# Image staging, constant loads and weight preparation moved in a four-layer pre-activation convolution kernel

## The chip, the core and the metric

The kernel runs on one core of a Trainium2 chip. The core has a tensor engine (PE, with its weight load PEld), a vector engine (DVE), a scalar engine (ACT), a general engine (POOL) and a sync engine (SP); SP, ACT and POOL can issue DMAs, each on a queue of its own. Each engine runs its own instructions in program order and waits on semaphores for the others. The metric is the device time of one execution in microseconds (us), lower is better.

## The reference

The input is x of 8 images, 128 channels, 96 x 96 pixels, float32. Four layers follow each other; each is the input plus a layer of its group norm (32 groups of 4 channels, statistics over 4 x 96 x 96 values of one image):

```python
x = x + dcnv4(_gn(x))            # layer 0
x = x + conv3x3(_gn(x), kernel)  # layer 1, 128 -> 128 channels
x = x + dwconv(ste_sign(v), w) + dwconv(v, ste_sign(w))   # layer 2, v = _gn(x), depthwise 3 x 3
x = x + scan(_gn(x))             # layer 3
```

Layer 0 is a deformable convolution: a depthwise 3 x 3 convolution of the normed image (x1), a norm of x1 over all channels and pixels, a gelu, and a projection that gives two offsets and a mask for each of 8 groups and 9 taps; each tap is then sampled bilinearly at its offset, weighted by the mask and summed. Layer 3 goes through the rows of an image from top to bottom: each row plus the last result goes through a 9-wide convolution over the row, a bias and a relu, and is the next carry.

## The kernel before

**Order of the work.** The layer-0 stage and the stage of layers 1 and 2 are not written in order. They make tasks for a planner (`Plan`, L96 on): a task has an engine, an estimated cost, what it depends on, a due time (`prio`), buffers that it uses and a `lag` until its result is there. `order` then simulates the engines: an idle engine takes the ready task with the lowest due time whose buffers are free. The instructions are emitted in that order, and on the chip each engine keeps it, whatever the real durations are. The engines carry on from one stage to the next without a barrier; only data, reused memory and the branch hold them.

**Start (L253 to L485).** `load_const` loads constants through ACT's DMA queue in the order of the code: 8 of them, then the small matrices `idq` and `gmq`, four more, and then for layer 0 the selection matrices `sel`, `shift`, `omb`, `omq` (8 loads), and the depthwise weights `dwq`, `dwbq`, `gnwq`, `gnbq`. DVE makes 18 diagonal matrices `dwd` from `idq` and `dwq`. POOL sets the edges of two image tiles `xqs` to zero.

**Layer 0 (L486 to L948).** The 128 partitions hold two row halves of 64 channels each, the channels' other half lies beside it (index j), so one image is a tile of 52 rows x 2 x 100 columns with a zero edge of 2; a row inside it is 96 values, 384 bytes, with gaps between rows. Two tiles alternate between images. `load_rows` (L483) issues four DMAs for a piece of rows: 24 DMAs for image 0, 48 for each later one, all on SP. Then `image` plans: `bn_stats` on DVE (L545, 24 of them), the aggregate, the means on PE, coefficients on DVE with a square root on ACT (L555 to L563, L329), and norms in place on ACT (L597, 26 pieces of 4 rows or less). The image is worked off in 12 bands of 4 rows per half. For a band the depthwise convolution gives x1: 36 matmuls on PE (L628), or, for bands 3, 5, 7 and 9 of image 0, 18 instructions on DVE (L620, L622); ACT takes it out of PSUM (L648), squares it for the statistics (L657), and SP stores it in DRAM (`x1d`, L665 and L669). When all 12 bands are done, the coefficients of x1's norm follow (L689 to L696, with a matmul by `amean`).

Then 12 chunks follow. For one chunk: x1 is loaded back (L731), gelu (L738), the projections (PE, L748), their eviction `o` (ACT, L767), tent functions of the offsets `h` (L757, L780), a check whether an offset is over 1 (`beyond`, L788, L793), the mask product (DVE, L809) and the residual row load `acc` (L821). Then come 9 weight products `wt` (POOL, L852) and 25 shifts, each with a selection (`select`, PE, L862, 4 matmuls into a PSUM buffer), a product with the shifted image (DVE, L879) and an addition, which is on PE into `ps_s` (L839), on POOL (L897) or on DVE (L886) by a fixed list. ACT writes the result y (L906) with sums for the next norm (L914), SP stores it (L919). PSUM has a pool "w" of three buffers that the bands, projections, selections and coefficients share, and one buffer `ps_s`. A band of the next image and its norms are planned among the chunks of the image before; for image 1 among those of image 0, and its bands start early. The loads of image 1 wait for the weights of layer 1: `conv_weights` (L502) loads `k1` into tile 1 of `xqs` and makes `km1` by six DVE sums, before image 1 may be loaded there.

**The flag (L949 to L959).** After the planned part, three DVE operations and a PE transpose reduce `beyond` to a flag, which is read into a register, and a branch (`tc.If`) follows. It guards a slow path for offsets over 1, which is not taken here.

**Layers 1 and 2 (L1093 to L1560).** The tiles of this stage have names with a suffix C, in chunks of 8 rows. Per image and chunk: y is loaded (L1241), normed (L1252), transformed over row pairs on POOL (`d`, L1259), multiplied with `km1` on PE (L1272, four products into two PSUM buffers `pv_C`) and summed into v on DVE (L1288 to L1308) with statistics (L1317). `v_coefs`, the norm of v (L1546) and `tap_chunk` follow for layer 2: nine taps are split over PE (L1385, L1392), DVE (L1406) and POOL (L1423), `xq` on POOL (L1362), the result `o` (L1467) is stored to `x3` (L1473), and `out_coefs` (L1494 to L1521) makes the coefficients of the last norm. `tap_weights` (L1132) makes sign and tanh of the taps on ACT and 20 small DVE operations; `late_weights` (L1153) loads the row weights `k3s` and makes `km` by six DVE sums. The due times of both lie in the first image: at 80 and 20 x 2 x `NCH`, but with no dependence, so the planner may take them when DVE or SP is idle before.

**Layer 3 (L1565 to L1692).** Suffix D, in groups of 4 rows of all images: `x3` is loaded in 24 groups of 1536 KB (`load`, L1626; groups 0 and 1 on POOL's queue before anything else, later ones on SP), normed (L1634), and each row in two halves of 4 images goes through a copy or sum (L1656, L1658), three transforms `tr` (L1660 to L1662), 36 matmuls (L1675), `m2` (L1683), `pair` (L1598 to L1601), a relu (L1614) and a POOL addition (L1615). The row result is the next row's carry, two halves alternate.

Memory is given to pools in order. A stage's pool lies where the closed pools of the stage before lay, and the first write to a piece waits for the last use of what lay there.

Of the kernel before, what the change touches and what calls it, by code (L numbers as in the profile page):

```python
# [11 lines left out]
F32 = mybir.dt.float32  # L12
I32 = mybir.dt.int32
AF = mybir.ActivationFunctionType
ALU = mybir.AluOpType
# [198 lines left out]
def kernel(  # L214
# [35 lines left out]
    def half(j):  # L250
        return slice(j * HC, (j + 1) * HC)
# [3 lines left out]

    def load_const(ap, shape, name):
        t = const.tile(shape, F32, name=name)
        nc.scalar.dma_start(t[:], ap)
        return t

    ident = load_const(c_ident, [P, P], "ident")
    gmean = load_const(c_gmean, [P, P], "gmean")
    amean = load_const(c_amean, [P, P], "amean")
    dww = load_const(dw_w, [P, K2], "dww")
    dwb = load_const(dw_b, [P, 1], "dwb")
    gnw = load_const(gn_w, [P, 1], "gnw")
    gnb = load_const(gn_b, [P, 1], "gnb")
    omw = load_const(om_wT, [P, 3 * GK], "omw")
# [8 lines left out]
    nc.vector.tensor_scalar(gmq[:], gmq[:], 1.0 / NB, None, ALU.mult)  # L277
    w2s = load_const(w2, [P, K2], "w2s")
    b3s = load_const(b3, [P, 1], "b3s")
    alx = load_const(alpha_x.unsqueeze(0).to_broadcast([P, 1]), [P, 1], "alx")  # L280
    alw = load_const(alpha_w.unsqueeze(0).to_broadcast([P, 1]), [P, 1], "alw")
    eps = const.tile([P, 1], F32, name="eps")
# [129 lines left out]
    with ExitStack() as ph:  # L412
# [16 lines left out]
        for j in range(NB):  # L429
            rows = slice(j * HC, j * HC + GR)  # L430
            taps = slice(j * GR, (j + 1) * GR)
            nc.scalar.dma_start(sel[rows, :, :], c_sel[taps, :, half(j)])
            nc.scalar.dma_start(shift[rows, :], c_shift[taps, :])
            with nc.allow_non_contiguous_dma(reason="216 biases, one per partition"):
                nc.scalar.dma_start(omb[rows, :], om_b[:, taps].rearrange("k r -> r k"))
            for b in range(NB):
                for m in range(NB):
                    nc.scalar.dma_start(
                        omq[half(b), j, :, m * HC : m * HC + GR],
                        om_wT[half(j), :].rearrange("c (k r) -> c k r", k=3)[:, :, m * GR : (m + 1) * GR],  # L440
                    )
            nc.scalar.dma_start(dwq[half(j), :, :], dw_w.rearrange("(j c) t -> c j t", c=HC))
            with nc.allow_non_contiguous_dma(reason="128 values of each"):
                nc.scalar.dma_start(dwbq[half(j), :], dw_b.rearrange("(j c) o -> c (j o)", c=HC))
                nc.scalar.dma_start(gnwq[half(j), :], gn_w.rearrange("(j c) o -> c (j o)", c=HC))
                nc.scalar.dma_start(gnbq[half(j), :], gn_b.rearrange("(j c) o -> c (j o)", c=HC))
# [5 lines left out]
        for xq in xqs:  # L452
            nc.gpsimd.memset(xq[:, :RS, :, :], 0.0)
            nc.gpsimd.memset(xq[:, XR - RS :, :, :], 0.0)
            nc.gpsimd.memset(xq[:, RS : XR - RS, :, :RS], 0.0)
            nc.gpsimd.memset(xq[:, RS : XR - RS, :, RS + W :], 0.0)
        nmx = wp.tile([P, N], F32, name="nmx")
# [18 lines left out]
        def load_rows(i, lo, hi):  # L476

            for b in range(NB):

                a, z = (max(lo, RS), hi) if b == 0 else (lo, min(hi, XR - RS))  # L480
                top = b * HB - RS
                for j in range(NB):
                    nc.sync.dma_start(  # L483
                        xqs[i % 2][half(b), a:z, j, RS : RS + W], x[i, half(j), top + a : top + z, :]
                    )  # L485
# [16 lines left out]
        def conv_weights(at):  # L502
# [10 lines left out]
                [], at, lag=4.0,  # L513
# [11 lines left out]
            return t  # L525

        def image(i, at):
# [13 lines left out]
            for m in range(NST):  # L541
                for j in range(NB):
                    stats.append(plan.task(
                        "DVE", 0.49,
                        lambda m=m, j=j: nc.vector.bn_stats(  # L545
                            st[:, j, m, :], xq[:, RS + m * RB : RS + (m + 1) * RB, j, RS : RS + W]
                        ),
                        [loads[m], loads[min(m + 1, NST - 1)]], at - 20 + m,
                    ))
# [45 lines left out]
            def norm(parts, lo, hi, j):  # L595
                rows = xq[parts, lo:hi, j, RS : RS + W]
                nc.scalar.activation(  # L597
                    rows, rows, AF.Identity, bias=bi[parts, j : j + 1], scale=sc[parts, j : j + 1]
                )
# [5 lines left out]

            st1 = small["st1"][:].rearrange("p (k c) -> p k c", k=2)
# [86 lines left out]
            def aggr1():  # L693
# [13 lines left out]
                [t], when, uses=[b3],  # L707
# [15 lines left out]
        def chunk(i, c, at, made):  # L723
# [37 lines left out]
            for k in (1, 0):  # L761
# [29 lines left out]
                plan.task(  # L791
# [5 lines left out]
                )  # L797
# [136 lines left out]

        squares = {}
        weights = conv_weights(-STEP * NST)
        made = {0: image(0, -STEP * NST)}
        for i in range(N):
            for c in range(NST):
                at = STEP * (i * NST + c)  # L940
                chunk(i, c, at, made[i])
            plan.task("DVE", 0.7, lambda i=i: y_stats(i), squares[i], at + 2 * STEP)
            if i + 1 < N:
                made[i + 1] = image(i + 1, STEP * i * NST)
        with tc.manual_schedule():
            plan.emit()


            m1 = sp.tile([P, 1], F32, name="m1")  # L949
            nc.vector.tensor_reduce(m1[:], beyond[:], AX.X, ALU.max)  # L950
            pt = plan.pools["s"].tiles[0]
            nc.tensor.transpose(pt[:1, 0, :P], m1[:], ident[:])
            m2 = sp.tile([1, 1], F32, name="m2")
            nc.vector.tensor_reduce(m2[:], pt[:1, 0, :P], AX.X, ALU.max)
            nc.vector.tensor_scalar(flag[:], m2[:], 0.0, None, ALU.is_gt)
# [146 lines left out]
    with ExitStack() as ph:  # L1102
        wp = ph.enter_context(tc.tile_pool(name="wpC", bufs=1))
# [7 lines left out]
        for name, n, shape in (  # L1111
# [4 lines left out]
            tiles = [wp.tile(shape, F32, name=f"{name}C{k}") for k in range(n)]  # L1116
# [15 lines left out]
        def tap_weights(at):  # L1132
# [13 lines left out]
            s = plan.task("ACT", 1.9, signs, [], at)  # L1146
# [6 lines left out]
        def late_weights(at):  # L1153

            ld = plan.task("SP", 0.6, lambda: nc.sync.dma_start(k3s[:], k3), [], at, lag=4.0)
# [373 lines left out]
        weights = tap_weights(20 * 4)  # L1529
        late_weights(20 * 2 * NCH)  # L1530
        for i in range(N):
# [6 lines left out]
            done = v_coefs(i, stats + ends.get(i - 2, []) + (weights if i == 0 else []), 20 * (i + 1) * NCH)  # L1538
            made[i] = [done]
            norms = []  # L1540
# [25 lines left out]
    with ExitStack() as ph:  # L1566

        wp = ph.enter_context(tc.tile_pool(name="wpD", bufs=1))
        xts = [wp.tile([P, N, LG, W], F32, name=f"xtD{g}") for g in range(3)]
        xgs = [wp.tile([P, N, LG, W], F32, name=f"xgD{g}") for g in range(3)]  # L1570
# [68 lines left out]
        with tc.manual_schedule():  # L1639
            for g in range(2):  # L1640
                load(g, nc.gpsimd)
# [122 lines left out]
```

## Time and profile before

| what | value |
| --- | --- |
| median of 3 runs | 5604.98 us (5604.57 to 5605.74) |
| the profiled execution | 5606.45 us, its span 5604.7 us |
| mean granted TensorE clock | 0.990 |
| PE, PEld | 96%, 54% of the span busy |
| DVE, ACT, POOL | 86%, 60%, 81% busy |
| layer-0 stage, by the last y | 0 to 3467.6 us |
| layers 1 and 2, by the last PE work | 3476.9 to 4822.1 us |
| layer 3 | from there to the end |

The profile is of one execution. A group row reads: line, engine, operation, output <- input (partitions x elements), count, then busy time and mean duration, and the idle time just before with what ended it. In a timeline a row has a start and a duration in us and a count if like instructions follow each other. In a row of a stretch each engine has its busy us with the number of its instructions, then the granted clock (1.00 is full), the DMA engines' share and the GB/s moved. Durations carry over to another kernel only for the same shape. The busy shares are averages over stages: what a stage is bound by has to be read in the stage.

### The profile page before, as it was taken

What the parts mean: (1) busy time and instruction counts of PE and PEld (TensorE: products, weight loads), DVE (VectorE), ACT (ScalarE), POOL (GpSimd) and SP (SyncE); (2) the same over time, 40 slices, a digit from 0 to 9 for tenths busy, and PEclk for the clock granted to TensorE, in tenths of its full rate; (3) what the DMA queues carried; (4) which work ended last, traced back from release to release, by engine and by line L of the source; (5) the groups of instructions that cost most, each with busy time, mean ns of one, the idle gap of its engine ahead of it and who ended that gap; (6) DMA issues with size and microseconds to landing.
All of it is one profiled execution on the core that took longest, in us unless ns stands there. A gap on an engine that the chain in (4) does not pass through costs nothing. (4 is left out here: it accounts for less than half of the span.)

```text
span 5604.7 us, 128829 instructions
## 1 busy us (share of the span) xinstructions
PE 5382.2 (96%) x53049; PEld 3007.8 (54%) x53049; DVE 4839.3 (86%) x6874; ACT 3371.5 (60%) x4816; POOL 4554.4 (81%) x2835
## 2 busy tenths in 40 slices
PE   5899999999999999999999998999999999899999
PEld 2354454454454454454454443545454554699999
DVE  5788888888888888888888998699999998688887
ACT  4656666656766666666666663477787777533333
POOL 0899999999999999999999998699999998422222
PEclk9999999999999999999999999999999999999999
DMA  6121121221212112112111111222222221223232
GB/s 128 48 60 58 54 61 58 56 61 58 56 59 60 54 58 61 55 59 60 46 49 47 43 41 40 61 67 64 66 67 67 65 66 48 83 95 109 94 110 80
DMA packets 423809, 360.65 MB, mean 64 GB/s; under 512 B 251889, under 2 KB 422417, under 8 KB 423217
## 3 DMA queue, kind: packets, MB, share of 16 engines
q1 hardware_dynamic: 390336, 310.33, 19.7%
q10 hardware_dynamic: 32144, 38.87, 2.0%
q8 instruction: 422, 6.91, 0.5%
q0 software_dynamic: 736, 3.15, 0.2%
q14 instruction: 171, 1.39, 0.1%
HBM read 201.26 MB, written 150.99 MB: 63 GB/s over the span
## 5 line engine op out<-in xcount | busy, mean ns | idle before, releaser
L862 PE MATMUL ps_w<-wt,sel 64*64 64x384 f32 x19200 | 1857.1, 488 | 58.7 <-DVE h L809 17.2
L879 DVE TENSOR_TENSOR pr<-ps_w,xq 128x768 f32<-128x768 f32 x1824 | 1670.0, 949 | 209.4 <-PE ps_w L862 158.7
L852 POOL TENSOR_TENSOR wt<-h,h 128x768 f32<-128x768 f32 x864 | 1583.9, 1838 | 262.1 <-DVE h L809 140.3
L897 POOL TENSOR_TENSOR acc<-acc,pr 128x768 f32<-128x768 f32 x882 | 1618.6, 1837 | 72.4 <-DVE pr L879 60.0
L862 PEld LDWEIGHTS ps_w<-wt,sel 64*64 64x64 f32 x19200 | 743.9, 133 | 925.3 <-issue 287.7
L1272 PE MATMUL pv_C<-dC,km 128*128 128x384 f32 x2304 | 776.2, 491 | 11.9 <-POOL dC L1259 5.0
L839 PE MATMUL ps_s<-pr,idq 64*64 64x384 f32 x7536 | 761.6, 484 | 1.7 <-DVE pr L879 1.1
L1406 DVE SCALAR_TENSOR_TENSOR ps_C<-xqC,w2s,ps_C 128x768 f32<-128x768 f32 x674 | 683.8, 1015 | 85.7 <-ACT ps_C L1444 70.9
L767 ACT ACTIVATE o<-ps_w,omb 128x768 f32<-128x768 f32 x192 | 172.7, 899 | 810.9 <-PE ps_w L748 705.8
L1615 POOL TENSOR_TENSOR xtD<-xtD,cr 128x384 f32<-128x384 f32 x192 | 192.0, 1000 | 575.2 <-ACT cr L1614 513.2
L628 PE MATMUL ps_w<-xq,dwd 64*64 64x384 f32 x6624 | 631.3, 487 | 13.3 <-ACT x L648 6.9
L1272 PEld LDWEIGHTS pv_C<-dC,km 128*128 128x128 f32 x2304 | 426.1, 189 | 359.1 <-issue 47.3
L879 DVE TENSOR_TENSOR ps_w<-ps_w,xq 128x768 f32<-128x768 f32 x480 | 459.9, 958 | 94.7 <-PE ps_w L862 93.5
L757 ACT ACTIVATE h<-o,shift 128x768 f32<-128x768 f32 x576 | 533.1, 926 | 11.1
L780 ACT ACTIVATE h<-h 128x768 f32<-128x768 f32 x576 | 485.8, 843 | 17.4
L1423 POOL TENSOR_TENSOR ptC<-ptC,ptC 128x768 f32<-128x768 f32 x255 | 476.6, 1869 | 1.1
L839 PEld LDWEIGHTS ps_s<-pr,idq 64*64 64x64 f32 x7536 | 307.3, 133 | 302.7 <-issue 164.3
L886 DVE TENSOR_TENSOR acc<-ps_w,acc 128x768 f32<-128x768 f32 x480 | 456.1, 950 | 6.7
L748 PE MATMUL ps_w<-x1c,omq 64*64 64x384 f32 x4608 | 434.7, 490 | 18.3 <-DVE pr L879 14.9
L628 PEld LDWEIGHTS ps_w<-xq,dwd 64*64 64x64 f32 x6624 | 279.1, 133 | 278.0 <-issue 122.0
L1675 PE MATMUL ps_b<-tr,km 128*128 128x192 f32 x2304 | 407.5, 325 | 16.5 <-DVE tr L1660 16.5
L1675 PE MATMUL ps_a<-tr,km 128*128 128x192 f32 x2304 | 406.2, 324 | 0.0
(198 smaller groups left out, 7165.0 us busy)
## 6 DMA issues: line engine op xcount, KB each, us to landing
ywC<-y SPq DMA_DIRECT2D x80, 480.0 KB, 3.9
acc<-in_x SPq DMA_DIRECT2D x192, 192.0 KB, 3.4
x1c<-x1d SPq DMA_DIRECT2D x192, 192.0 KB, 3.3
y<-y SPq DMA_DIRECT2D x96, 384.0 KB, 3.3
x<-oC SPq DMA_DIRECT2D x192, 192.0 KB, 2.8
out<-xtD ACTq DMA_DIRECT2D x24, 1536.0 KB, 5.7
x1d<-x SPq DMA_DIRECT2D x92, 384.0 KB, 2.8
xtD<-x SPq DMA_DIRECT2D x22, 1536.0 KB, 7.0
```

The source lines that it names most:

```text
L628: nc.tensor.matmul(ps.tile[half(j), b, :FB], dwd[half(b), j, t, :], xq[half(b), r0 : r0 + RB, j, c0 : c0 + W], start=(t == 0), stop=(t == ...
L757: nc.scalar.activation(h, o, AF.Abs, bias=shift[:, k * NR + r : k * NR + r + 1])
L780: lambda h=h: nc.scalar.activation(h.tile[:], h.tile[:], AF.Relu, bias=1.0, scale=-1.0),
L839: nc.tensor.matmul(total.tile[half(j), b, :FB], idq[half(b), :], pr.tile[half(b), j, :], start=first, stop=last)
L852: lambda wt=wt, hy=hy, hx=hx: nc.gpsimd.tensor_tensor(wt.tile[:], hy.tile[:], hx.tile[:], ALU.mult),
L862: nc.tensor.matmul(ps.tile[half(b), j, :FB], sel[half(j), n, :], wt.tile[half(j), b, :], start=True, stop=True)
L879: nc.vector.tensor_tensor(view(pr.tile), view(ps.tile), x_s, ALU.mult)
L897: lambda pr=pr, acc2=acc2: nc.gpsimd.tensor_tensor(acc2.tile[:], acc2.tile[:], pr.tile[:], ALU.add),
L1272: nc.tensor.matmul(flat(ps), km1[:, k, x_, :], d.tile[:, k, :, x_ : x_ + W], start=(x_ == 0), stop=(x_ == 2))
L1406: nc.vector.scalar_tensor_tensor(view, rows8(src, t), w[:, t : t + 1], view, ALU.mult, ALU.add)
L1423: lambda a=parts[0], b=pt: nc.gpsimd.tensor_tensor(a.tile[:], a.tile[:], b.tile[:], ALU.add),
L1675: nc.tensor.matmul(ps[:, at_f : at_f + nf], km[:, k, t, :], tr[:, par, :, v : v + HW2], start=(t == 0), stop=(t == NT - 1),)
```

## The change

- Image 0 is loaded without gaps into the memory of tile 1 (`stage`, rows of one half and one j one behind the other), the statistics read it there, and the norms go from there to tile 0. Tile 1's edge is set to zero later, in a POOL task after `conv_weights`, which now waits for the norms of image 0; the loads of image 1 wait for that POOL task.
- 29 constants are no longer loaded through ACT's queue at once; they are SP tasks with a due time just behind image 0's loads. `dwb`, `idq`, `gmq`, `dwq` and `dwbq` stay on ACT. The first `amean` matmul waits for all 29 in the planner.
- The flag's operations become tasks that depend on the last checks, so they go out as soon as those are done.
- In the stage of layers 1 and 2, the tiles yw, d, sg and th get a pool of their own, which is opened first. `tap_weights` waits for the statistics of chunk 3 of image 0, `late_weights` for v's coefficients of image 2 (the third).
- In layer 3, the tiles `xtD0`, `xgD0` and `xtD1` lie in a pool that is opened first, thus where the pool named above was. Group 0 is loaded on POOL's queue, group 1 on SP's.

```diff
+    late = []
+
+    def put_off(to, ap):
+        def load():
+            with nc.allow_non_contiguous_dma(reason="a few values per partition"):
+                nc.sync.dma_start(to, ap)
+
+        late.append(load)
+
     def load_const(ap, shape, name):
         t = const.tile(shape, F32, name=name)
-        nc.scalar.dma_start(t[:], ap)
+        put_off(t[:], ap)
         return t
...
-            nc.scalar.dma_start(sel[rows, :, :], c_sel[taps, :, half(j)])
-            nc.scalar.dma_start(shift[rows, :], c_shift[taps, :])
...
+            put_off(gnwq[half(j), :], gn_w.rearrange("(j c) o -> c (j o)", c=HC))
+            put_off(gnbq[half(j), :], gn_b.rearrange("(j c) o -> c (j o)", c=HC))
+            put_off(shift[rows, :], c_shift[taps, :])
+            put_off(omb[rows, :], om_b[:, taps].rearrange("k r -> r k"))
...
+            put_off(sel[rows, :, :], c_sel[taps, :, half(j)])
...
-        for xq in xqs:
+
+        def zero_edges(xq):
...
+        zero_edges(xqs[0])
+
+        stage = xqs[1][:].rearrange("p r j w -> p (r j w)")[:, : NB * XR * W].rearrange("p (j r w) -> p j r w", j=NB, w=W)
...
+                    rows = x[i, half(j), top + a : top + z, :]
+                    if i == 0:
+                        nc.sync.dma_start(
+                            stage[half(b), j, a:z, :].rearrange("p r w -> p (r w)"), rows.rearrange("p r w -> p (r w)")
+                        )
+                    else:
+                        nc.sync.dma_start(xqs[i % 2][half(b), a:z, j, RS : RS + W], rows)
...
-                [], at, lag=4.0,
+                before, at, lag=4.0,
...
-            return t
+            return t + [plan.task("POOL", 2.5, lambda: zero_edges(xqs[1]), t, at)]
...
-                    rows, rows, AF.Identity, bias=bi[parts, j : j + 1], scale=sc[parts, j : j + 1]
+                    rows,
+                    rows if i else stage[parts, j, lo:hi, :],
...
-                [t], when, uses=[b3],
+                [t, *constants], when, uses=[b3],
...
-        squares = {}
-        weights = conv_weights(-STEP * NST)
-        made = {0: image(0, -STEP * NST)}
+        squares, checks = {}, []
+        constants = [plan.task("SP", 0.6, load, [], -STEP * NST - 29, lag=3.0) for load in late]
+        made, normed = {}, {}
+        made[0] = image(0, -STEP * NST)
+        weights = conv_weights(-STEP * NST + 40, normed[0])
...
+        def set_flag():
+            nc.vector.tensor_reduce(m2[:], pt.tile[:1, 0, :P], AX.X, ALU.max)
+            nc.vector.tensor_scalar(flag[:], m2[:], 0.0, None, ALU.is_gt)
+
+        t = plan.task("DVE", 0.35, lambda: nc.vector.tensor_reduce(m1[:], beyond[:], AX.X, ALU.max), checks, -1e6)
+        t = plan.task("PE", 0.4, lambda: nc.tensor.transpose(pt.tile[:1, 0, :P], m1[:], ident[:]), [t], -1e6, uses=[pt], lag=0.1)
+        plan.task("DVE", 0.45, set_flag, [t], -1e6, uses=[pt])
...
+        wx = ph.enter_context(tc.tile_pool(name="wx", bufs=1))
         wp = ph.enter_context(tc.tile_pool(name="wpC", bufs=1))
...
+            pool = wx if name in ("yw", "d", "sg", "th") else wp
+            tiles = [pool.tile(shape, F32, name=f"{name}C{k}") for k in range(n)]
...
-        weights = tap_weights(20 * 4)
-        late_weights(20 * 2 * NCH)
...
+            weights = tap_weights(20 * 6, stats[CB * 3 : CB * 4]) if i == 0 else []
...
+            if i == min(2, N - 1):
+                late_weights(20 * (i + 1) * NCH + 40, made[i])
...
+        wx = ph.enter_context(tc.tile_pool(name="wxD", bufs=1))
+        size = [P, N, LG, W]
+        xts, xgs = [wx.tile(size, F32, name="xtD0")], [wx.tile(size, F32, name="xgD0")]
+        xts.append(wx.tile(size, F32, name="xtD1"))
...
-            for g in range(2):
-                load(g, nc.gpsimd)
+            load(0, nc.gpsimd)
+            load(1)
```

## The prediction, before the changed kernel ran

> **What bounds the kernel now.** I read the page first (PE busy 96% of the span), then the timeline and the busy times by stretch at the places that the change touches: the first 204 us, the seam at 3470 us and the seam at 4822 us. The chain of waits starts only at 3476 us, so for the beginning I followed the timeline by hand. Columns of the timeline: start, duration, engine, line, what, and in brackets the idle time before it and what ended it.
>
> ```profile
> 0.74 40.46 SPq L483 DMA_DIRECT2D xq<-in_x  x24
> ...
> 47.60 2.40 DVE L545 BATCH_NORM_STATS2 st<-xq 128x6 f32<-128x384 f32 x5 [0.91 <-DMA xq<-in_x]
> ...
> 55.73 12.54 ACT L597 ACTIVATE xq<-xq,bi,sc 64x192 f32<-64x192 f32 x21 [0.89 <-DVE bi L329]
> ```
> The first image takes 24 DMAs of about 192 KB, issued every 1.69 us; the statistics wait for the data until 47.6, and norming starts at 55.73. Call that moment S.
>
> ```profile
> 93.00:96.00 3.00, 0.00 (x0) 0.00 (x0) 2.93 (x6) 2.66 (x6) 0.00 (x0) 0.74 1.02 196
> 96.00:99.00 3.00, 2.80 (x20) 1.23 (x24) 2.93 (x6) 1.18 (x4) 0.00 (x0) 0.50 1.13 280
> ...
> 153.00:156.00 3.00, 0.99 (x8) 0.30 (x8) 1.92 (x2) 2.97 (x5) 0.00 (x0) 0.50 0.00 0
> ```
> Stretches with busy us and counts of PE, PEld, DVE, ACT, POOL, then granted clock, DMA share, GB/s. During the first image's convolution DVE is full; PE falls idle, then runs at half clock. In 147 to 171 (last row) PE is nearly idle at half clock.
>
> ```profile
> 148.67 1.56 PE L862 MATMUL ps_w<-wt,sel 64*64 64x384 f32 x8 [1.09 <-ACT o L767]
> ...
> 203.85 0.81 ACT L906 ACTIVATE y<-ps_s 128x768 f32<-128x768 f32 x1 [6.54 <-PE ps_s L839]
> ```
> The first chunk needs 55.2 us from first select to its y. Later y follow each other by 29.6 to 42 us, with the same pattern in every image: PE and POOL are then full.
>
> ```profile
> 3492.62 7.66 PE L1272 MATMUL pv_C<-dC,km 128*128 128x384 f32 x23 [2.92 <-DVE vn L1288]
> ...
> 4828.64 1.93 POOL L1626 DMA_DIRECT2D xtD<-x  x2 [8.89 <-DVE bi L329]
> ...
> 4832.00:4834.00 2.00, 0.00 (x0) 0.00 (x0) 0.00 (x0) 0.00 (x0) 0.00 (x0) 0.50 1.06 394
> ...
> 4843.66 4.18 PE L1675 MATMUL ps_b<-tr,km 128*128 128x192 f32 x12 [16.53 <-DVE tr L1660]
> ```
> At 3492 PE waits for a DVE that is busy with k3's weights. At the last seam everything waits 11 us for a load that is issued only after the coefficients.
>
> **First image (gain 26.2).** The rows move at 384 B each; 44 to 48 us shows 208 GB/s, while the 1536-byte rows of 4832 reach 394. In contiguous form they are 3072 B or more. The program's order shows that a queue waits for the eighth DMA before, so the landing also depends on what shares these slots: before, tiny constants on ACT's queue (4 omq loads took 5.88 us to issue). They leave. I take the issue interval that 192 KB loads have elsewhere (x1c: 1.24 for 2): 24 x 0.65 + 0.7 = 16.3, and 4.5 to land: 20.8. The Trainium skill (DMA: Bandwidth & Descriptors, "Measured") speaks against this: single transfers of 64 KB reach 138 GB/s, of 1 MB 341, so 192 KB estimated at 200, hence 4.9 MB in 25 us, landing 27. But 208 GB/s was reached here with 384-byte rows, several loads in flight; I keep 20.8, and 27 for the range. DVE then: 18 diagonals end near 13.3, 22 statistics x 0.475 = 10.4, so 23.8; bn_aggr 0.8; the coefficients took 4.2 with the k1 sums in between, about 3.9 without. S = 28.5, rounded up to 29.5 for waits on the ACT constants; landing at 27 would make it 34.6. Gain 55.7 - 29.5 = 26.2 (21 to 27).
>
> The 29 deferred constants go on SP behind the image. Their issues took about 23 us on ACT; from 16.5 that ends at 40, the four residual loads at 43 to 45. SP is next needed for the first x1d store, at S + 13.6 = 43: about covered; beyond that, each us is a us of SP.
>
> **Convolution and the second image (loss 3.6).** Times from S. DVE's band 3 starts at 5.4 as before (61.16 - 55.73), 10.9 a band (1.39 + 16 instructions in 9.55). Band 5 waits for its PSUM buffer until 20.4. The k1 load now waits for the last norm (74.1 before: 18.4) and, behind x1d and x1c on SP, issues near 20; k3's equal load took 6.0, so 26. DVE reaches it at 25.3: stall 0 to 2. Six sums, 2.9. Band 5 ends at 35.7. Bands 7 and 9 then alternate in two PSUM buffers, 22.7: to 58.4, and band 7 is evacuated only at 57.7. PE's last two bands wait for that buffer. They are 144 rows of 0.0807 = 11.6. Rule of the Trainium skill (TensorE: Matmul & The Clock Gate, "What's actually happening"): about 3.4 us idle halves the clock, 3.4 us busy restores it, costing an estimated 1.7. The row at 96.20 had 200 in 18.92, against 16.1 at full clock: 2.8. I take the row's: PE ends at 72.2, against 62.6 before (118.35).
>
> Then evacuation to coefficients as before, 7.7: 79.9. gelu and the first tents need 14.5: 94.5. Meanwhile SP: edges are zeroed on POOL at 38 (8 memsets were 2.35, here half), 48 loads x 0.65 interleaved with x1d stores that wait for evacuations; the last land near 89. Behind them in DVE's queue stand ten statistics, then the mask products: 91. So the first select can start at 96.5. The table loads for Sqrt and back (1.28 each) lie on ACT. Before: 92.9. Loss 3.6 (from -2 to +12).
>
> **First chunk (gain 19.2).** Before, two bands of the second image held two of three PSUM buffers from 122 to 169, since ACT normed late; each select cost 2.64 us. These bands now come after. DVE's work is 25 x 0.93 + 5 x 0.95 + 3 masks 2.9 + 1.2 = 32; with a cold start 36, against 55.2. Bounds 33 and 45.
>
> **Given back (loss 6.5).** Two bands of PE, 11.6 us, move into full chunks; 300 to 400 us holds 1236 PE rows x 0.0807 = 99.8. Chunks 0 to 3 of the first image took 97.97, of the third 103.4: 5.4 less where these bands were done ahead. I take 6.5; bounds 3 and 12. From chunk 5 the program's orders agree up to the last image, so nothing else repeats.
>
> **Seam at 3470 (gain 2).** Three flag operations (0.34, 0.28, 0.14) and a transpose leave the tail: the branch follows y_stats at 3470.74 instead of 3472.0. But DVE does their 0.76 in a full chunk: net 0.5 (0 to 1.3). Without k3 and its sums (6 operations, 3486.4 to 3491.95) DVE releases the product at 3487, and PE's 2.92 goes. Next late would be PE itself. The sums return in the third image, 5.7 us on a DVE with 4 of 50 us free: cost 1 (0 to 4); the 20 small tap operations (3.3 us) fit gaps of 1.25 between products, cost 0.4. Net 1.5 (-2 to 2.9). The inserted table load runs on an ACT that waits anyway; uncovered 1.28.
>
> **Seam at 4822 (gain 11.5).** POOL issues load 0 after its last xq at 4812.2, SP load 1 the same time, ahead of six x stores on SP (2.8 us to land each; oC has two buffers). Three of POOL's last four additions stand behind the DMA, about 1 us; PE needs them at 4820.6: 0.3 late. Both loads land near 4822 at 380 GB/s. The coefficients still end at 4827.9; then norms 2.51, copy and sum 1.0: PE at 4832 instead of 4843.7. PE idles 5 us, so it starts cold as before. Bounds 8 and 13.
>
> **Sum.** 26.2 - 3.6 + 19.2 - 6.5 + 0.5 + 1.5 + 11.5 = 48.8. The profiled execution took 5606.45 (span 5604.7 and 1.75 around it), so 5557.6; the median of the runs lies 1.5 below it: 5556.
>
> **Rivals.**
> 1. *The second image takes back.* Its statistics stand ahead of masks in DVE's queue; loads that land 12 later and a give-back of 12 cost 14 more, a slower landing 5: gain 30, 5575. For: SP's stores stand between its loads. Against: ACT's tents need 94.5 anyway.
> 2. *All cover holds.* First select at 91, chunk 33, give-back 3, S 28.5: 13 to 14 more, 5542.
> 3. *The image doesn't come faster*: eight outstanding DMAs set the pace, not their rows. S stays near 55: gain 23, 5582. Against: 192 KB land in 2.8 to 3.3 us elsewhere.
> 4. *Slower: constants clog SP.* They stand ahead of x1d stores, whose two buffers hold ACT and so every band. At 0.8 us each they are covered; each further 1 us costs 29. Above 2.5 us each (omq's worst is 1.47) the whole 49 are lost; at 3.0, 64 are: 5620.
>
> **How the numbers follow.** Main case 55% (alone 5547 to 5566), rival 1 23%, rival 2 13%, rival 3 4%, rival 4 5%: 2% of it slower, 3% within 0.2% (11 us, about what a measurement of this kernel can tell from no change). Range 5540 to 5580.
>
> **What would show it.** S near 29.5; first select near 126 and first y near 162; the second y's distance over 36; no k3 wait at the seam; PE of the last stage starting about 10 us after the last PE work of the stage before (4822.05 to 4843.66, 21.6, now). Wrong if S exceeds 40, if the image's loads keep 1.69 us, or if SP is still on constants past 50.

## The result, and the profile after

The changed kernel takes 5584.07 us (median of 6 runs, 5575.73 to 5587.12), the kernel before 5603.67 in the same runs (5596.16 to 5605.74): 19.6 us less, ratio 0.9965 with a 95% interval of 0.9954 to 0.9976. The forecast was 5556 with a range up to 5580: the gain has the sign that was forecast and 0.4 of the size. The profiled execution of the changed kernel took 5575.73 (span 5574.0) and is the fastest of the six, so its spans flatter the change by some us; the end of this section says where.

The timeline of the changed kernel's start (start, duration, engine, line, what; in brackets the idle time before it and what ended it):

```profile
0.75 19.20 SPq L499 DMA_DIRECT2D xq<-in_x  x24
...
28.57 2.40 DVE L563 BATCH_NORM_STATS2 st<-xq 128x6 f32<-128x384 f32 x5 [1.05 <-DMA xq<-in_x]
...
35.65 12.49 ACT L618 ACTIVATE xq<-xq,bi,sc 64x192 f32<-64x192 f32 x21 [0.63 <-DVE bi L339]
...
126.67 1.56 PE L888 MATMUL ps_w<-wt,sel 64*64 64x384 f32 x8 [0.43 <-DVE h L835]
...
172.42 0.79 ACT L932 ACTIVATE y<-ps_s 128x768 f32<-128x768 f32 x1
```

The image's 24 DMAs are issued in 19.2 us instead of 40.5, the last statistics run behind 28.57, and the first norm starts at 35.65 (before: 55.73, forecast: 29.5). The first selection comes at 126.67 (148.67; the forecast's path gives 126), the first y at 172.42 (203.85; forecast 162). Up to the last y of image 0 (556.1 against 580.5) the lead shrinks from 31.4 to 24.3 us.

The last seam, first two lines of the kernel before (ACT), then the timeline of the changed kernel:

```profile
4807.56 2.58 ACT L1414 ACTIVATE ptC<-vn,wsg 128x768 f32<-128x768 f32 x3
...
4840.05 4.89 ACT L1634 ACTIVATE xgD<-xtD,bi,sc 128x384 f32<-128x384 f32 x8 [12.62 <-DMA xtD<-x]
```

```profile
4773.64 2.58 ACT L1448 ACTIVATE ptC<-vn,wsg 128x768 f32<-128x768 f32 x3
...
4778.65 1.05 POOL L1665 DMA_DIRECT2D xtD<-x  x1 [0.30 <-POOL xqC L1402]
...
4789.50 4.29 ACT L1673 ACTIVATE xgD<-xtD,bi,sc 128x384 f32<-128x384 f32 x7 [13.28 <-DMA xtD<-x]
4793.70 0.79 ACT L1501 ACTIVATE oC<-ps_C 128x768 f32<-128x768 f32 x1
...
4794.54 3.94 PE L1419 MATMUL ps_C<-vn,dgv 64*64 64x384 f32 x24 [14.81 <-ACT oC L1501]
...
4812.93 4.18 PE L1714 MATMUL ps_b<-tr,km 128*128 128x192 f32 x12 [2.90 <-DVE tr L1699]
```

Read it from below. PE starts the last stage after only 2.9 us of idling (16.53 before), which looks like success. But the stage before it ended late: PE stood 14.81 us, waiting for an eviction oC on ACT, and that eviction came right behind seven norms xgD of the last stage (before, all eight norms came behind the last eviction). These wait 13.28 us for group 0's load, which POOL had issued at 4778.65. The early load itself works; what waits for it stands in front of the stage that is not finished. To compare kernels I take the distance from the group "ptC x3" on ACT, which lies ahead of the tail in all of them, to the last stage's first matmul: 36.1 us before (4807.56 to 4843.66), 39.3 after (4773.64 to 4812.93).

| step, by the two profiles | forecast | measured |
| --- | --- | --- |
| first norm | +26.2 | +20.1 (55.73 to 35.65) |
| from there to the first selection | -3.6 | +1.9 (92.9 to 91.0) |
| first selection to first y | +19.2 | +9.4 (55.18 to 45.75) |
| given back up to image 0's last y | -6.5 | -7.1 |
| last y of layer 0 to ptC x3 | +2.0 | +3.4 (1339.95 to 1336.59) |
| ptC x3 to the last stage | +11.5 | -3.2 (36.1 to 39.3) |
| sum | 48.8 | 24.5 |

What the profiles show beyond the sum, 6.2 us between image 0's last y and layer 0's, is not put down to the change. Layer 0's last y fell at 3437.05 in this profile; in five experiments below that leave layer 0 as in the changed kernel (e1, e2, e7, e10, e13) it fell at 3444.07 to 3447.69. The difference lies where one image follows another, with up to 2.4 us at each such place. There PE waits for DVE ahead of a projection; these are two of these places in the profile of before:

```profile
1439.97 2.84 PE L748 MATMUL ps_w<-x1c,omq 64*64 64x384 f32 x16 [3.61 <-DVE pr L879]
```

```profile
2285.86 1.52 PE L748 MATMUL ps_w<-x1c,omq 64*64 64x384 f32 x16 [0.46 <-DVE pr L879]
```

In the profiles the wait is either about 3.6 us, and then 16 matmuls take 2.84 us (granted clock 0.50 from 1440 to 1442), or half a us, and they take 1.52 (clock 1.00). From the last y of the image to the next it takes 42.0 us in the first case (1425.7 to 1467.7) and 39.7 in the second (2273.8 to 2313.5). Profiles of kernels that are alike in layer 0 so differ by up to 10.6 us; that the spread of one kernel's runs (9.6 and 11.4 us) has the same cause is likely, but not shown. I therefore read the experiments by the stage that they touch, in particular at the last y of image 0, which lies ahead of all these places.

### The profile page after: what moved, and what is told of

It is laid out like the page before. It is cut to its first block, busy times and chain, and to the rows that moved or that the text cites. A ratio compares the mean times of both kernels' runs of the same rounds, so it can differ in the third digit from the quotient of the medians.

```text
span 5574.0 us, 128853 instructions
## 1 busy us (share of the span) xinstructions
PE 5375.0 (96%) x53049; PEld 3013.9 (54%) x53049; DVE 4837.6 (87%) x6874; ACT 3376.3 (61%) x4820; POOL 4552.6 (82%) x2834
## 3 DMA queue, kind: packets, MB, share of 16 engines
q1 hardware_dynamic: 386096, 312.91, 19.6%
```

## Experiments

Times are medians, each beside runs of the kernel before on the same chip (5604.3 to 5605.7). "Image 0's last y" is 580.5 before and 556.1 in the changed kernel.

**Norms held (e1).** Group 0's norms read copies of the coefficients that DVE makes after the last ones.

```diff
+            for to, of in zip(held, (bi3, sc3)):
+                nc.vector.tensor_copy(to[:], of[:])
...
+            bi, sc = held if g == 0 else (bi3, sc3)
```

> The changed kernel, but the eight norms of group 0 of the last stage read copies of the coefficients that are made after the last image's, so that ACT cannot have them ahead of its last evictions. From the eviction group ptC x3 on ACT to the last stage's first matmul it took 36.1 us before (4807.56 to 4843.66) and 39.3 us after the change (4773.64 to 4812.93). Theory A (the queue): seven norms stand in ACT's order ahead of the last three evictions, and so the whole tail waits for the load; without that the early load is worth what was forecast: about 25 us, the kernel 14 us faster than the changed one, near 5570. Theory B (the load itself costs: it holds POOL and shares the DMA engines with the last stores): 36 us or more, and the time within 3 us of the changed kernel's 5584.

5577.3 us (ratio 0.9951, 0.9937 to 0.9965). The tail, in its timeline:

```profile
4783.48 2.58 ACT L1448 ACTIVATE ptC<-vn,wsg 128x768 f32<-128x768 f32 x3
...
4788.22 0.38 SPq L1666 DMA_DIRECT2D xtD<-x  x1
...
4801.59 0.81 ACT L1501 ACTIVATE oC<-ps_C 128x768 f32<-128x768 f32 x1 [5.17 <-DMA x<-oC]
...
4812.74 4.18 PE L1718 MATMUL ps_b<-tr,km 128*128 128x192 f32 x12 [5.83 <-DVE tr L1703]
```

The distance is 29.3 us, 10 less than in the changed kernel, so the queue order (A) cost at least that. It isn't the 25 of theory A: with the norms gone, the last eviction waits 5.17 us for the store that must free its buffer, and that store lies behind both loads: issued at 4789.34, it releases the eviction only at 4801.5, 12 us later, where such a store lands in 2.8 us elsewhere (the 6.3 us that the next expectation names are those of the stores after it). Theory B thus names a second, smaller cost. The arrangement is now the one that the forecast had in mind, both loads early and all norms behind the coefficients, and it gains 6.8 us (36.1 to 29.3), less than the forecast's lower bound of 8.

**One early load (e7).** As in e1, and group 1's tile stays in the later pool, so that only group 0 is loaded early.

```diff
-        xts.append(wx.tile(size, F32, name="xtD1"))
         wp = ph.enter_context(tc.tile_pool(name="wpD", bufs=1))
-        xts.append(wp.tile(size, F32, name="xtD2"))
+        xts += [wp.tile(size, F32, name=f"xtD{g}") for g in (1, 2)]
```

> As the run with held norms, but the tile of group 1 stays in the later pool, so that only group 0's 1.5 MB are loaded early. There the last eviction but none waited 5.17 us for a store that lay behind the two loads (6.3 us to land in place of 2.8), and ptC x3 to the last stage's first matmul took 29.3 us (36.1 before, 39.3 changed). Theory B2 (the second load holds the stores): 24 to 25 us, and 4 to 5 us faster than with held norms. Theory B1 (the first load holds them as well): 27 us or more.

5571.0 us (0.994, 0.9926 to 0.9953).

```profile
4798.55 0.81 ACT L1501 ACTIVATE oC<-ps_C 128x768 f32<-128x768 f32 x1 [2.31 <-PE ps_C L1426]
...
4809.40 3.79 PE L1717 MATMUL ps_b<-tr,km 128*128 128x192 f32 x12 [5.83 <-DVE tr L1702]
```

The last eviction no longer waits for a store but for PE. The distance is 26.1 us: 3.2 of the 5.17 come back, between the two theories.

**Early norms (e10).** One early load, and the copies are made right behind the last aggregate, for the first seven images.

```diff
+                if i == N - 1:
+                    for to, of in zip(held, (bi3, sc3)):
+                        nc.vector.tensor_copy(to[:, : N - 1], of[:, : N - 1])
...
+            bi, sc = held if g == 0 and i < N - 1 else (bi3, sc3)
```

> The changed kernel with one early load (group 1's tile in the later pool) and with the norms of group 0 reading copies of the first seven images' coefficients, which DVE makes right behind the last aggregate: three norms then stand ahead of the last square root on ACT and none ahead of the last evictions. With one load and all norms behind the coefficients it took 26.1 us from ptC x3 (4783.30) to the last stage's first matmul (4809.40); 5.1 of it lay between the last coefficients and that matmul. Theory A with B (queue order and the stores are all that was lost): 22 to 24 us, 5565 to 5569. Against: the row tiles' memset and the copy on DVE still follow the coefficients, so no more than 3 us; if ACT's square root is held by the load, 27 us or more.

5568.69 us (0.9935, 0.9921 to 0.9948); the distance is 24.1 us (4784.70 to 4808.79).

```profile
4802.70 1.90 ACT L1677 ACTIVATE xgD<-xtD,bi3d,sc3d 128x384 f32<-128x384 f32 x3 [1.95 <-DVE sc3d L1532]
...
4808.79 4.12 PE L1718 MATMUL ps_b<-tr,km 128*128 128x192 f32 x12 [3.51 <-DVE tr L1703]
```

Three norms now lie beside the coefficients' own chain. 36.1 - 24.1 is 12.0, near the 11.5 that the forecast took for this seam. The agreement is in part luck: 2.0 of it come from norms beside the coefficients, which the forecast did not have, and one load has stayed late.

**The old last stage (e2).** Both pools and both loads as before, the rest changed.

```diff
-        wx = ph.enter_context(tc.tile_pool(name="wxD", bufs=1))
...
-            load(0, nc.gpsimd)
-            load(1)
+            for g in range(2):
+                load(g, nc.gpsimd)
```

> The changed kernel with the last stage's part undone (one pool in each of the two last stages, both first loads on POOL's queue). Theory A: the distance from ptC x3 to the last stage's first matmul is 36 us as before, so 3 us faster than the changed kernel, near 5581. Theory C (the seam did gain 11.5 us as forecast and the gain was lost elsewhere in the stage): 11 us slower, near 5595.

5583.41 us (0.996, 0.9946 to 0.9974), distance 36.06: theory A, by the trace. 3 us are too little to be seen in the medians.

**Gaps (e3) and constants on ACT (e4).** Each undoes one half of the new start.

```diff
-                    if i == 0:
-                        nc.sync.dma_start(
-                            stage[half(b), j, a:z, :].rearrange("p r w -> p (r w)"), rows.rearrange("p r w -> p (r w)")
-                        )
-                    else:
-                        nc.sync.dma_start(xqs[i % 2][half(b), a:z, j, RS : RS + W], rows)
+                    nc.sync.dma_start(xqs[i % 2][half(b), a:z, j, RS : RS + W], rows)
```

```diff
-                nc.sync.dma_start(to, ap)
+                nc.scalar.dma_start(to, ap)
...
-        late.append(load)
+        load()
```

> The changed kernel, but image 0 goes with gaps into its own tile, as before, and is normed in place; the constants stay behind it. The first norm starts at 35.65 in the changed kernel, at 55.73 before. Theory R (the length of the rows made the load faster): the first norm near 50, the kernel 12 us slower than the changed one. Theory K (the constants' leaving made it faster, since the image came at 220 GB/s without gaps and at 180 to 208 with them): the first norm at 36 to 39, 0 to 3 us slower.

> The changed kernel, but all constants are loaded at once through ACT's queue, as before; image 0 comes without gaps. Theory R: the first norm within 4 us of 35.65 and the time within 4 us of the changed kernel's. Theory K: the first norm at 46 or later, the kernel 10 us or more slower.

With gaps: 5590.55 us (0.9974, 0.9965 to 0.9984), image 0's last y at 565.1. With the constants on ACT: 5598.49 (0.999, 0.9984 to 0.9997), last y at 570.2. First the gaps' timeline, then that of the constants:

```profile
41.71 12.55 ACT L611 ACTIVATE xq<-xq,bi,sc 64x192 f32<-64x192 f32 x21 [0.61 <-DVE bi L339]
```

```profile
49.15 12.49 ACT L618 ACTIVATE xq<-xq,bi,sc 64x192 f32<-64x192 f32 x21 [0.62 <-DVE bi L339]
```

And the stretch 12 to 16 us with gaps, then in the changed kernel (us and counts of PE, PEld, DVE, ACT, POOL, granted clock, DMA share, GB/s):

```profile
12.00:16.00 4.00, 0.00 (x0) 0.00 (x0) 4.00 (x19) 0.00 (x0) 0.00 (x0) 1.00 1.30 176
```

```profile
12.00:16.00 4.00, 0.00 (x0) 0.00 (x0) 3.77 (x15) 0.00 (x0) 0.00 (x0) 1.00 1.05 220
```

Of the 20.1 us at the first norm, 14.0 belong to the constants (55.73 to 41.71, with the later k1 sums in it) and 6.1 to the rows without gaps (41.71 to 35.65); undone from the other side they are 13.5 and 6.6. Theory K is right in the main (it wanted the first norm at 36 to 39 with gaps), theory R for a third: the 384-byte rows move at 176 GB/s, the 3072-byte ones at 220, not at the 300 that the forecast's issue interval comes to. How the constants hold the image back is seen in what SP's queue waits for ahead of the image's DMAs. In the profile of before the longest are (us in total, times, longest):

```profile
SPq L483 <- DMA omb<-in_om_b: 4.3, 1, 4.3
SPq L483 <- DMA omq<-in_om_wT: 4.1, 5, 1.3
SPq L483 <- DMA shift<-in_c_shift: 4.1, 1, 4.1
```

Before, SP waits 20.3 us for constants and 2.1 for earlier pieces of the image; with the constants on ACT (e4) it is 16.5 and 3.4, in the changed kernel 2.4 and 2.1. The DMA engines are not full meanwhile: in e4 their share is 0.39 from 28 to 32 us, in the changed kernel 1.05 from 12 to 24. So the image was held at its issue, by the slots that the forecast had named in passing.

**Short pieces (e12) and both halves in one DMA (e5).** What holds the image at 220 GB/s? The first takes 1536-byte pieces in the same number of DMAs, the second one DMA for both row halves.

```diff
+                if i == 0:
+                    nc.sync.dma_start(
+                        stage[half(b), :, a:z, :].rearrange("p j r w -> p j (r w)"),
+                        x[0].rearrange("(j c) h w -> c j (h w)", c=HC)[:, :, (top + a) * W : (top + z) * W],
+                    )
+                    continue
...
-            step = 1 if i else 2
+            step = 1
```

```diff
+                    rows = x[0, half(j)].rearrange("c (b h) w -> b c (h w)", b=NB)
+                    nc.sync.dma_start(
+                        stage[:, j, a:z, :].rearrange("p r w -> p (r w)"), rows[:, :, (a - RS) * W : (z - RS) * W]
+                    )
...
```

> The changed kernel, but image 0's 24 DMAs of about 192 KB take both channel halves of one band (pieces of 1536 bytes for 64 partitions) in place of one half of two bands (3072 bytes). The one DMA for both row halves only reached 51 GB/s at a DMA share of 0.13, so it could not tell what bounds the 220 GB/s. Theory P (64 partitions bound the rate): the image at 200 to 230 GB/s again, the first norm at 34 to 37, time within 2 us. Theory L (long pieces are slow, 1536 bytes are not: the last stage's 390 GB/s is of such): the image lands by 16 to 20, the first norm at 28 to 31, the last y of image 0 5 us earlier, time near 5579.

> The changed kernel, but image 0's interior rows are loaded by one DMA for both row halves (128 partitions, 12 DMAs of 384 KB and four small ones for the edge rows) in place of 64 partitions each. In the changed kernel the image came at 220 GB/s with all 16 DMA engines busy, while the last stage's loads to 128 partitions reach 370 to 400. Theory P (64 partitions are what halves the rate): the image lands by about 18, the statistics on DVE then bound the start, the first norm at 29 to 30, first image's last y 5 us earlier, near 5579. Theory Q (the rate belongs to the input or to the many rows, not to the number of partitions): the first norm at 35 to 37 as before, time within 2 us of the changed kernel.

Short pieces: 5584.21 us (0.9964, 0.995 to 0.9977), first norm at 34.66. Both halves: 5654.23 (1.0087, 1.0073 to 1.0101), first norm at 104.58. A stretch of each, short pieces first:

```profile
12.00:16.00 4.00, 0.00 (x0) 0.00 (x0) 3.92 (x14) 0.00 (x0) 0.00 (x0) 1.00 1.09 234
```

```profile
32.00:36.00 4.00, 0.00 (x0) 0.00 (x0) 1.48 (x3) 0.00 (x0) 0.00 (x0) 1.00 0.13 51
```

The length of the pieces is not it, between 1536 and 3072 bytes: 234 GB/s with all engines busy. Both halves in one DMA turned into another experiment: a DMA whose source runs first over the two halves uses 0.13 of the DMA engines, about two of 16, and moves 51 GB/s. So it doesn't say whether 64 partitions bound the rate; e12 leaves that theory standing, and it stays open.

**The first chunk: bands later (e6), fewer additions on POOL (e8), norms later (e9).**

```diff
-                when = at + STEP * (1 + c * (NST - 3) / (NST - 1)) + DW_SLOT
+                when = at + STEP * (1 + c * (NST - 3) / (NST - 1)) + DW_SLOT + (1.5 * STEP * (1 - c / (NST - 1)) if i == 1 else 0)
```

```diff
-                    who = (ADDERS[c % len(ADDERS)] if i < N - 1 else LAST_ADDERS)[slot]
+                    who = (ADDERS[c % len(ADDERS)] if i < N - 1 and (i, c) != (0, 0) else LAST_ADDERS)[slot]
```

```diff
-                    "ACT", 0.55 if a[2] - a[1] == RB else 0.35, lambda a=a: norm(*a), [coefs], at + 4 + 1.5 * k
+                    "ACT", 0.55 if a[2] - a[1] == RB else 0.35, lambda a=a: norm(*a), [coefs], at + 4 + 1.5 * k + (30 if i == 1 else 0)
```

> The changed kernel, with the convolution bands of image 1 due 37 us later at the first band, falling to nothing at the last, so that they leave the first chunk. In the changed kernel the first chunk takes 45.7 us from first selection (126.67) to y (172.4), with POOL full from 133 to 164 and PE full nearly as long. Theory G (POOL bounds it: some 20 additions and products of 1.83 us): the first chunk within 2 us of 45.7. Theory H (72 matmuls of the bands and cold PE bound it): 5 us or more shorter. In both the last y of the first image, 556.1, stays within 2 us, since the bands have to be done anyway.

> The changed kernel, but the first chunk of the first image spreads its additions by the list of the last image (fewer on POOL, more on PE). Theory G (POOL bounds the first chunk): 4 to 6 us off its 45.7 us, the last y of the first image 2 to 5 us earlier. Theory H (PE bounds it): the first chunk 1 to 3 us longer.

> The changed kernel, with the norms of image 1 on ACT due 30 us later. In every run so far ACT was full from 124 to 172, in the first chunk (7.8 of 8 us), also where the bands were taken out of it (first chunk 48.7) and where POOL had fewer additions (51.7), and the chunk did not get shorter in either. Theory J (ACT bounds the first chunk: tents, checks and image 1's norms): 38 to 41 us from first selection to y in place of 45.7. Theory K2 (several engines take turns, none alone bounds it): 44 us or more. The last y of image 0 moves by less than 3 us in both, since the norms have to be made anyway.

| | first selection to first y | image 0's last y | median (ratio, interval) |
| --- | --- | --- | --- |
| changed | 45.7 | 556.1 | 5584.07 (0.9965, 0.9954 to 0.9976) |
| bands later | 48.7 | 561.9 | 5589.92 (0.997, 0.9958 to 0.9982) |
| fewer on POOL | 51.6 | 553.7 | 5580.44 (0.9954, 0.9941 to 0.9968) |
| norms later | 44.2 | 553.3 | 5579.89 (0.9952, 0.9937 to 0.9968) |

These numbers need the spread of kernels that are alike here. Where this part is as in the changed kernel, the first column is either 45.8 us (e1, e5, e14) or 48.0 to 48.4 (e2, e3, e4, e7, e10, e12, e13), and image 0's last y lies from 555.3 to 557.3 (e1, e2, e7, e10, e13, e14). The stretch 132 to 140 shows the difference, first in the changed kernel (followed by a later stretch of it), then in e2:

```profile
132.00:140.00 8.00, 6.92 (x88) 3.52 (x88) 7.66 (x9) 7.83 (x11) 6.76 (x4) 0.99 0.01 2
...
148.00:156.00 8.00, 8.00 (x104) 4.49 (x100) 6.00 (x8) 7.90 (x13) 8.00 (x5) 1.00 0.05 15
```

```profile
132.00:140.00 8.00, 8.00 (x68) 3.15 (x68) 5.65 (x7) 7.87 (x13) 7.54 (x5) 0.67 0.01 2
```

Among the profiles with this start the granted clock is 0.67 to 0.72 there in the longer case (e2, e7, e10, e12, e13) and 0.99 or 1.00 in the shorter one (changed, e1, e14).

Bands later: the edit did not do what it was made for. The first band's 72 matmuls stay in the first chunk (148.2 to 157.6; 147.7 to 157.1 in the changed kernel); only the later bands move. So theory H is not tested, 48.7 is the longer case (clock 0.71), and the bands are missing further on: the last y comes 4.6 us or more later than in all kernels that are alike. Fewer additions on POOL: theory G wanted 4 to 6 us less; it became 3 to 6 more, so G fell, and the sign is that of H (1 to 3 more). Norms later: 18 norms instead of 25 are in the first chunk, and it is 1.6 us shorter, not 5 to 8 as theory J wanted. But ACT is as full as before (47.2 us of the 48 from 124 to 172, 46.1 in the changed kernel), since other tasks take the room, so J is not refuted either. What bounds the first chunk stays open. Fewer additions on POOL and later norms both bring image 0's last y forward, by 1.6 to 4 us.

**The seam at 3440: weights (e13) and flag (e14) at their old places.**

```diff
+        weights = tap_weights(20 * 4, [])
+        late_weights(20 * 2 * NCH, [])
...
-            weights = tap_weights(20 * 6, stats[CB * 3 : CB * 4]) if i == 0 else []
...
-            if i == min(2, N - 1):
-                late_weights(20 * (i + 1) * NCH + 40, made[i])
```

```diff
-        t = plan.task("DVE", 0.35, lambda: nc.vector.tensor_reduce(m1[:], beyond[:], AX.X, ALU.max), checks, -1e6)
+        t = plan.task("DVE", 0.35, lambda: nc.vector.tensor_reduce(m1[:], beyond[:], AX.X, ALU.max), checks + [last], -1e6)
```

> The changed kernel with the preparation of the tap weights and of the row weights at its old place in the stage of layers 1 and 2. From the last y of layer 0 to the eviction group ptC x3 it took 1339.95 us before and 1336.59 after the change. Theory W (the weights' move made it): 1339 or more, and PE waits again for DVE near 16 us into the stage. Theory F (the flag's move made it): within 1 us of 1336.6.

> The changed kernel with the flag's operations made to wait for the last image's y statistics, so that they stand at the end of layer 0 again. Theory F: from the last y to the first matmul of the next stage 8.2 us or more (9.36 before, 6.84 after the change). Theory W: within 0.5 us of 6.84. The forecast took 1.3 us for the operations that leave the tail; the profile shows 2.5.

Old weights: 5585.89 us (0.9966, 0.9955 to 0.9978); last y to ptC x3 1336.63, as in the changed kernel. Old flag: 5589.75 (0.997, 0.9959 to 0.9981); last y to the next stage's first matmul 9.15 instead of 6.84. First the old weights, then the old flag:

```profile
3465.88 24.43 PE L1306 MATMUL pv_C<-dC,km 128*128 128x384 f32 x75 [2.57 <-DVE vn L1322]
```

```profile
3454.47 0.98 PE L1243 MATMUL pv_C<-ymv,gmean 128*128 128x1 f32 x4 [5.44 <-DVEq L991]
```

The 2.57 us wait for DVE is back with the old weights, and still the stage ends no later: at the new place the same sums have to be made too. They stand in the fourth image's convolution there; from its first matmul by `km1` to the fifth image's it takes 163.6 us in the changed kernel (163.4 to 164.7 in the other experiments), 161.7 with the old weights and 162.1 before. So most of what the seam wins is paid there. The flag's move is worth 2.3 us (6.5 to 6.8 in all kernels that have it, 9.15 and 9.36 in the two that do not). The distance to ptC x3 differs by up to 3 us between kernels that are alike in this stage (1336.6 to 1339.9), so more than these 2.3 can't be given to anything here.

**Together (e11).** Early norms with one early load (e10), later norms of image 1 (e9) and fewer additions on POOL (e8).

> The changed kernel with three of the edits together: one early load and early norms in the last stage (alone 5568.7, before in the same runs 5604.3), image 1's norms 30 us later (the last y of image 0 at 553.3 in place of 556.1), and the first chunk's additions by the last image's list (553.7). If the two edits in the first chunks are worth their 2.5 us each beside each other: the last y of image 0 near 551, the kernel near 5564. If both only use the same idle time: near 553.5 and 5566.

5562.06 us (0.9925, 0.9912 to 0.9939), image 0's last y at 553.3. By the last y the two edits of the first chunk use the same idle time; one of them is enough. This version is faster than both kernels; against the changed one the ratios' intervals don't meet.

## Why the prediction was wrong

**The last seam, 14.7 us: the step that failed.** It said "The coefficients still end at 4827.9; then norms 2.51", and took for granted that the norms come behind the coefficients on ACT as they did before. There, however, the load was issued only behind the coefficients. The norms of seven images need nothing but their own image's coefficients and the load. In the code they stand behind the whole stage of layers 1 and 2, but with the load early, seven of them are ahead of that stage's last three evictions in ACT's order; the program's order shows that before any run. The forecast counted what the moved load waits for and what waits on POOL and SP behind it, but not its readers. Instead of a gain of 11.5 us the seam lost 3.2. Holding the norms takes it from 39.3 to 29.3 us, and e10 to 24.1. It also named the six stores on SP and gave them no price; with two loads early they cost up to 5.2 us, of which 3.2 came back with one. This step alone takes the time out of the range: with the seam as in e7 or e10 the kernel takes 5571.0 or 5568.69 us, the other misses unchanged.

**The first image, 6.1 us.** "I keep 20.8" for the landing was wrong; the last wait of the statistics for the image ends at 28.57, and S at 35.65 lies 1 us beyond the bound of that step (34.6). The size failed, and the reason with it: that the rows' length decides. The 208 GB/s by which it kept 20.8 was misread: in 44 to 48 us k1's load was under way as well (issued at 41.24, awaited until 50.44); in the two stretches of 4 us before, it is 180. Most of the gain (14.0 of 20.1) is the constants' leaving, which the forecast had as a side remark (the slots). The estimate that it had worked out from the Trainium skill (DMA: Bandwidth & Descriptors, "Measured"), 200 GB/s for 192 KB, was nearer to the 220 than the row of the last stage, whose loads go to 128 partitions.

**The first chunk, 9.8 us.** "DVE's work is ... 32; with a cold start 36" took one engine. From 124 to 172 us of the changed kernel ACT is busy for 46.1 us of 48, POOL for 41.9, PE for 41.5 and DVE for 38.1: DVE is the least full of the four. What came, 45.7, is just over the upper bound that it gave (45), and kernels that are alike took up to 48.4. The wanted comparison was in the profile of before: from an image's last y to the first of the next, with the same bands and norms in it, take 39.5 to 42.0 us. "These bands now come after" is wrong too: 72 of their matmuls are in the first chunk. What they cost there, no run shows.

**Right.** The first selection (126 forecast, 126.67), but by two errors that cancel, which is luck: S 6.1 later, the convolution 5.5 shorter. 3.9 of these 5.5 are there when PE's last two bands start (53.9 us from S, 57.7 forecast). The two bands cost 14.38 us (89.53 on), as the row of the half clock said (11.6 + 2.8). Given back 7.1 (6.5). The constants were not in SP's way: they took 0.33 to 0.91 us each and the last was issued by 41.5, ahead of the first x1d store at 49.72, so rival 4 fell. Of the 2 us at the seam behind layer 0, the flag had 2.3 and the weights nothing that can be told from the spread (0.5 and 1.5 forecast).

**The signs and the rivals.** The first selection, the second y's distance (36.5), the k3 wait that is gone and PE's start 8.0 us after the last PE work of the stage before all came as named; S and the first y did not. The last of these could not show the failure: PE's work of the stage before ended late itself. The measured time is that of rival 3, but not by its cause: S did fall. Rival 1 fell with the first selection. Rival 2 had the 91 us from S to the first selection right, but S, the first chunk and the give-back are above its numbers. None of them had an engine's queue order at the last seam.

## What to carry to other kernels

When a transfer is moved ahead, its readers can move too: look on every engine's order at what now stands behind them, and hold them by a dependence on something late. A chunk in which four engines are each nearly full isn't forecast from one of them; take the nearest like chunk of the trace. Before a gain is given to the shape of a transfer, look at what shares its slots: undoing one half at a time is cheap.

## What the runs showed of the hardware

- A DMA whose source's outermost dimension was 2 ran at 51 GB/s with a DMA share of 0.13; the same bytes in DMAs of 64 partitions ran at 220 with 1.05.
- To 64 partitions 384-byte rows moved at 176 GB/s, 1536-byte pieces at 234, 3072-byte ones at 220, all with full engines (DMA shares 1.30, 1.09 and 1.05); the last stage's 1.5 MB loads to 128 partitions at 372 to 394 (4832 to 4838 us of the kernel before). Why, was not found.
- At the end of an image PE waited either near 0.5 us, and the next 16 matmuls took 1.52 us at clock 1.00, or near 3.6 us, and they took 2.84 at clock 0.50; from one image's last y to the next y it took 39.7 and 42.0 us. Over layer 0 profiles of kernels that are alike there differ by up to 10.6 us.
